# A selective-scan block with two layer norms and a linear attention: C's tails fetched a slot later, output offsets added two slots behind their products, a norm's third square kept out of two slots

## The chip, the cores and the metric

The kernel runs on one core of a Trainium2 chip. A core has a matrix engine (TensorE, PE in the profile; PEld is its loading of weights), a vector engine (DVE), an activation engine (ACT), a general engine (GpSimd, POOL) and a sync engine (SP), which here issues nearly all DMA transfers. Each engine works through its own instructions in order; semaphores order them against each other. The metric is device time in microseconds (us) of the whole kernel, median of several executions. Slot, step and group are the program's own words, explained below.

## The reference

The input x is 4 x 512 x 64 x 64. Two layers, each added to its input, each behind a group norm over 16 channels. The first is a Mamba block on four chunks of 128 channels; the second is a linear attention with 8 heads. Cut to what matters here:

```
def step(h, inp):                                   # 4096 positions, in order
    dt_t, B_t, C_t, x_t = inp
    dA = jnp.exp(dt_t[:, :, None] * A)
    h = dA * h + (dt_t * x_t)[:, :, None] * B_t[:, None, :]
    y = jnp.einsum('bds,bs->bd', h, C_t)            # 16 states, 256 channels
    return (h, y)
...
y = y * silu(z);  ym = out_proj(y) + skip * chunk
y = layer_norm(ym); x = x + y @ proj_w.T + proj_b
...
kq = einsum('bnhc,bnhd->bhcd', relu(k), relu(q))    # summed over all 4096 positions
out = (v @ kq / norm) @ w_out.T + b_out; x = x + out
```

## The kernel before

**Tiles and steps.** A tile is one batch element's 512 positions (32 tiles). A step is one chunk of 128 channels of a tile: 128 steps in order of batch, tile, chunk. A step has 256 inner channels (two halves `e`) of 16 states each; it is cut into 16 slots. Two slots, an even one (`jj` 0) and an odd one (`jj` 1), form a group: 4 states by 32 channels on the 128 partitions, four blocks of 32 channels next to each other in the free dimension, 512 positions each. There are 2,048 slots and 1,024 groups.

**A slot** (`slot`, from L835). POOL makes the drive `bx` = dt x times B for the slot after next (`drive`, L833). DVE runs two scans over time (L851); ACT makes the next decays `dA` (L825). In an even slot DVE multiplies the group before, its first 384 positions, by C out of PSUM (`product`, L871), and PE folds the states into `y` (`fold_states`). The last 128 positions, C's tail, are multiplied on POOL at the end of the odd slot (L863), behind the copy of the last state (L862), by `c_sb`, a broadcast of rows of C out of DRAM.

**Fetches.** `b_row` (even slots) issues four DMAs of 64 KB that broadcast the rows of B of the group three groups ahead; its tile has three buffers, so it waits until POOL's drives have read the old one. `c_tail` issues four DMAs of 16 KB for a tail; its tile `c_sb` has two buffers, so one may be filled while the other is read. Before the change it is called in the odd slot for the group that follows. Both issue through `for_states` (L800). SP also issues, from the `after` part of a slot, the spreads of dt and dt x (`spread`, two DMAs of 256 KB in each of slots 0 to 3 and 8 to 11, L752), the rows of dt (L739), of B and C (L771, L772), the 1 MB loads and stores of x tiles (L148, L542, L584) and the output's stores (L1144).

**After.** `after` is what a slot does besides: work with a fixed slot number, work put off by `later(n, ...)` until n slots on, and one piece each of three queues of generators: `ahead` (the norms before the scan), `late` (`leave`: the second layer norm and projection of a finished tile) and `rest` (the attention of a finished batch). A generator gives back a word at each `yield` that says when it may go on. `clear` holds a generator while the slot is one of `AWAY` (3 and 10, where ACT has the softplus and the silu with their table loads) or while more than one long ACT pass has been put into this slot. `room` holds it while PSUM work banks are taken: `held` counts them, and the limit is one in slots 1 to 5 and two elsewhere. The word "two ahead" is let through in slots 0, 1, 6 to 8 and 15.

**The norm behind the scan** (`layer_scale`). Four squares on ACT (L519), `part(0)` to `part(3)`, whose sums PE takes two by two. There is a `clear` before the first two and before the fourth; the third, `part(2)`, follows the sums of the first two at once.

**The attention's offset.** For batches 0 to 2, PE makes for each of four groups of output channels a product of 16 matmuls with one column (`pob`) in a work bank, and `offset` (L1102) adds it to the bias on DVE and frees the bank; it is put off by `later`. Behind all four come small additions on POOL (L1138), and then the attention's output (`pr`, stored through L1142). The last batch's attention runs behind the loop, in a branch of its own.

Of the kernel before, what the change touches and what calls it, by code (L numbers as in the profile page):

```python
# [24 lines left out]
def kernel(  # L25
# [53 lines left out]
    def work_bank(name, behind=1):  # L79
        held[0] += behind  # L80
        return ps_w.tile([P, T], F32, tag="w", name=name)

    def free(n=1):
        held[0] -= n

    def later(n, what):

        done = []

        def both():  # L90
            what()
            done.append(True)

        if now[0] is None:
            both()
        else:
            due.append((now[0] + n, both))
        return done
# [5 lines left out]
    def until(*done):  # L104
        while not all(done):
            yield "wait"

    def clear():

        while now[0] is not None and (now[0] % SLOTS in AWAY or passes[0] > 1):  # L110
            yield "wait" if now[0] % SLOTS in AWAY else "free"
# [4 lines left out]
    def room(when="wait"):  # L116

        while now[0] is not None and held[0] >= limit[0]:
            yield when
# [6 lines left out]
    def mm(out_, lhsT, rhs, abreast=1, **how):  # L126

        work["mm"] += (0.25 if rhs.dtype == BF16 else 1.0) * rhs.shape[-1] / T / abreast
        nc.tensor.matmul(out_, lhsT, rhs, **how)  # L129
# [276 lines left out]
    def bc(v, n):  # L406
        return v.unsqueeze(1).to_broadcast([P, n, v.shape[-1]])


    def sums_into(sums, parts, cs):  # L410
        for c in cs:
            mm(
                sums[c * LANE : (c + 1) * LANE, :], ones.to_broadcast([P, LANE]), parts[c],
                start=True, stop=True, abreast=len(cs),
            )

    def mean_of(sums, what, when, stop=True):

        got = wk.tile([P, T], F32, tag="sq", name=f"got_{what}", bufs=4)

        def take():
            nc.scalar.copy(got, sums)
            free()

        copied = later(1, take)
        yield
        yield from until(copied)
        yield when
        yield from room(when)
        bank = work_bank(what)  # L430
        mm(bank, mean.to_broadcast([P, P]), got, start=True, stop=stop)
        return bank
# [9 lines left out]
    def over_deviation(v, var, name):  # L442
        rs = wk.tile([P, T], F32, tag="sq", name=f"rs_{name}", bufs=4)

        def root():
            nc.scalar.activation(rs, var, AF.Ln, bias=eps)
            nc.scalar.activation(var, rs, AF.Exp, scale=-0.5)

        rooted = later(1, root)
        yield  # L450
        yield from until(rooted)
        yield "wide"
        over(v, var, ALU.mult)
        free()
        norming.clear()
        yield
# [38 lines left out]
    def layer_scale(v, name):  # L495


        while norming:
            yield "wait"
        norming.append(name)  # L500
        yield from room()
        sums = work_bank(f"mu_sums_{name}")
        sums_into(sums, [v[:, c, :] for c in range(NC)], range(NC))
        mu = yield from mean_of(sums, f"mu_{name}", None)
        mu2 = wk.tile([P, T], F32, tag="sq", name=f"mu2_{name}", bufs=4)

        def square():
            nc.scalar.activation(mu2, mu, AF.Square, bias=about)
            free()

        squared = later(1, square)
        yield
        yield from until(squared)
        sqs = [None] * NC

        def part(c):
            sqs[c] = wk.tile([P, T], F32, tag="sq", name=f"sq_{name}_{c}", bufs=4)
            passes[0] += 1
            nc.scalar.activation(sqs[c], v[:, c, :], AF.Square, bias=about)  # L519

        yield from clear()
        part(0)
        part(1)
        yield
        yield from room()
        sums = work_bank(f"var_sums_{name}")
        sums_into(sums, sqs, (0, 1))
        part(2)
        yield "free"
        yield from clear()  # L530
        part(3)
        yield "free"
        sums_into(sums, sqs, (2, 3))
        var = yield from mean_of(sums, f"var_{name}", "two ahead", False)
        mm(var, minus_first.to_broadcast([P, P]), mu2, start=False, stop=True)
        yield from over_deviation(v, var, name)
# [252 lines left out]
    def place(g):  # L789

        n, r = divmod(g, SLOTS)
        e, r = divmod(r, NQ * JJ)
        return n, e, *divmod(r, JJ)
# [3 lines left out]
    def for_states(dst, rows_, q):  # L797

        for k in range(KS):
            nc.sync.dma_start(  # L800
                dst[k * BLK : (k + 1) * BLK, :], rows_[q * KS + k, :].partition_broadcast(BLK)
            )

    def b_row(g):
        n, e, q, _ = place(g)
        b_all[g // JJ] = wk.tile([P, T], F32, tag="b_all", name=f"b_all_{g}", bufs=3)
        for_states(b_all[g // JJ], fs[n]["b_rows"], q)

    def c_tail(g):
        n, e, q, _ = place(g)  # L810
        c_sb[g // JJ] = wk.tile([P, T - CUT], F32, tag="c_sb", name=f"c_sb_{g}", bufs=2)
        for_states(c_sb[g // JJ], fs[n]["c_rows"], q)
# [7 lines left out]
    def decay(k):  # L820

        n, e, q, jj = place(k // 2)
        j = jj * 2 + k % 2
        dAs[k] = ps_d.tile([P, T], F32, tag="dA", name=f"dA_{k}")
        nc.scalar.activation(  # L825
            dAs[k], fs[n]["d_all", e][:, 0, j, :], AF.Exp, scale=a_t[:, e, j, q : q + 1]
        )

    def drive(g):

        n, e, q, jj = place(g)
        bxs[g] = wk.tile([P, 2, T], F32, tag="bx", name=f"bx_{g}", bufs=3)
        nc.gpsimd.tensor_tensor(  # L833
            bxs[g], fs[n]["d_all", e][:, 1, jj * 2 : jj * 2 + 2, :], bc(b_all[g // JJ], 2), ALU.mult
        )  # L835

    def slot(g, last, after):
        n, e, q, jj = place(g)
        b, t, c = steps[n]
        if g + 2 < last:  # L840
            drive(g + 2)
        if jj == 0:
            if g + 3 * JJ < last:
                b_row(g + 3 * JJ)
            hs[g // JJ] = wk.tile([P, NJ, T], F32, tag="h", name=f"h_{g}", bufs=2)
        elif g + 1 < last:
            c_tail(g + 1)
        h = hs[g // JJ]
        for i in range(2):
            j = jj * 2 + i  # L850
            nc.vector.tensor_tensor_scan(  # L851
                h[:, j, :], dAs.pop(2 * g + i), bxs[g][:, i, :],
                0.0 if t == 0 else st[:, c, e, q, j : j + 1], ALU.mult, ALU.add,
            )
            if 2 * g + i + LEAD < 2 * last:
                decay(2 * g + i + LEAD)
            if i == int(g % SLOTS == AWAY[1]) and jj == 0 and g:
                product(g - 1)
                fold_states(g - 1, last)
        del bxs[g]  # L860
        if jj == JJ - 1:
            nc.gpsimd.tensor_copy(st[:, c, e, q, :], h[:, :, T - 1])  # L862
            nc.gpsimd.tensor_tensor(  # L863
                h[:, :, CUT:], h[:, :, CUT:], bc(c_sb.pop(g // JJ), NJ), ALU.mult
            )
        after()

    def product(g):

        own = hs[g // JJ][:, :, :CUT]  # L870
        nc.vector.tensor_tensor(own, own, bc(c_all.pop(g // JJ), NJ), ALU.mult)  # L871
# [51 lines left out]
    def attention(b, x1s, stats):  # L923
# [5 lines left out]
        last = b == B - 1  # L929
# [123 lines left out]
        taken = []  # L1053
# [8 lines left out]
        for p in range(NC):  # L1062
            yield from room()
            pm = work_bank(f"pm2_{b}_{p}")
# [8 lines left out]
        taken = []  # L1073
# [10 lines left out]
        for m in range(NC):  # L1084
            yield from room()
            pm = work_bank(f"pm3_{b}_{m}")
# [12 lines left out]
        taken = []  # L1099

        def offset(o, pm):
            nc.vector.tensor_tensor(ob[:, o : o + 1], pm[:, 0:1], bo[:, o : o + 1], ALU.add)  # L1102
            free()
# [12 lines left out]
        for o in range(0 if last else NC):  # L1116
            yield from room()
            pm = work_bank(f"pob_{b}_{o}")
            for p in range(NC):
                mm(  # L1120
                    pm[:, 0:1], m2[:, p, o * P : (o + 1) * P], bv[:, p : p + 1],
                    start=(p == 0), stop=False,
                )
            for m in range(NC):
                mm(
                    pm[:, 0:1], m3[:, m, o * P : (o + 1) * P], ngm[:, m : m + 1],
                    start=False, stop=(m == NC - 1),
                )
            taken.append(later(1, lambda o=o, pm=pm: offset(o, pm)))
            yield  # L1130
        yield from until(*taken)
        free_x()
# [120 lines left out]
    wide, taken = 0, []  # L1253
# [208 lines left out]
```

## Time and profile before

| what | us |
|---|---|
| median of three runs | 7667.04 |
| the three runs | 7658.92 to 7670.27 |
| the profiled execution's own time | 7665.56 |
| its span, first to last instruction | 7663.9 |
| POOL: the drives, L833 | 4825.1 |
| POOL: the tails' product, L863 | 1301.2 |
| DVE: scans, L851 (both forms) | 4351.8 and 591.4 |
| DVE: product with C, L871 | 1771.0 |
| ACT: decays, L825 | 2752.5 |
| ACT: the squares of the norm behind the scan, L519 | 85.8 |

In a line for a group of instructions the columns are: source line, engine, operation, the tiles written and read, the shapes, the count, then busy time and the mean duration in ns of one, then the idle time of that engine just before such an instruction, and what ended most of it. In a line of the waits: who waited, for whom, the total in us, how many times, the longest. In the timeline: start, duration, engine, line, operation, tiles; in brackets the idle time before it and what ended it. A `q` after an engine's name means its sequencer, which issues transfers and waits.

### The profile page before, as it was taken

Reading aid. Unit: us, or ns where it says so; the run is one execution under the profiler, and the core shown is the slowest. Engines: PE = TensorE matmul, PEld = TensorE weight load, DVE = VectorE, ACT = ScalarE, POOL = GpSimd, SP = SyncE. Lnnn points to the kernel's source line nnn. Section 1 sums busy time; section 2 is a strip of 40 time slices with the busy share of each in tenths; the row PEclk is TensorE's granted clock in tenths of the full one; section 3 lists DMA queues with packets and bytes.
Section 4 is the critical chain, followed back from the end, with each engine's and each line's share of the span. In section 5 each row is a group of like instructions: output and inputs, shape, how many; then the busy total and the mean of one; then the engine's idle time right before and its main releaser. Section 6 shows DMA issues by size and latency. Waiting matters only on the chain.

```text
span 7663.9 us, 93895 instructions
## 1 busy us (share of the span) xinstructions
PE 6445.6 (84%) x25507; PEld 2129.9 (28%) x25528; DVE 6950.2 (91%) x5720; ACT 5455.4 (71%) x8384; POOL 6890.5 (90%) x4638
## 2 busy tenths in 40 slices
PE   5677777777798899998788889898789999899799
PEld 2122222121232233332222233332223333233244
DVE  6999999999999999899999999999999999999821
ACT  5677777777777777777777777777777777777521
POOL 5999999999999999999999999999999999999700
PEclk8787877787899999999799999999889999999899
DMA  6666666666666666676666666667676666677502
GB/s 173 170 172 165 160 152 162 161 162 167 178 168 167 168 172 167 170 195 181 172 178 171 177 168 170 162 177 209 164 169 166 163 160 162 172 189 192 146 34 93
DMA packets 829233, 1265.55 MB, mean 165 GB/s; under 512 B 184072, under 2 KB 317720, under 8 KB 816416
## 3 DMA queue, kind: packets, MB, share of 16 engines
q1 hardware_dynamic: 806352, 1225.99, 61.6%
q0 software_dynamic: 16368, 32.51, 2.5%
q8 instruction: 204, 3.34, 0.2%
q14 instruction: 325, 2.66, 0.1%
q10 hardware_dynamic: 5984, 1.06, 0.1%
HBM read 1052.25 MB, written 206.57 MB: 164 GB/s over the span
## 4 chain that ended last, share of the span: by engine, by line
PE 28%; DVE 23%; DMA 13%; ACT 12%; issue 9%; POOL 9%; SPq 5%; POOLq 0%; DVEq 0%; ACTq 0%
DVE h L851 14%; DVE h L871 7%; PE pc L129 7%; POOL bx L833 6%; ACT dA L825 5%; DMA d_all<-d_rows 5%; DMA c_sb<-c_rows 4%; PE pq L129 4%; PE y L129 4%; SPq L800 4%; PE pp L129 3%; PE pr L129 3%; PE po L129 2%; DMA b_all<-b_rows 2%; DVE xn L440 2%
## 5 line engine op out<-in xcount | busy, mean ns | idle before, releaser
L833 POOL TENSOR_TENSOR bx<-d_all,b_all 128x1024 f32<-128x1024 f32 x2048 | 4825.1, 2369 | 105.5 <-DVE h L851 85.9
L851 DVE TENSOR_TENSOR_SCAN h<-dA,st,bx 128x512 f32<-128x512 f32 x3584 | 4351.8, 1267 | 252.7 <-PE y L129 99.0
L825 ACT ACTIVATE dA<-d_all,a_t 128x512 f32<-128x512 f32 x4096 | 2752.5, 687 | 1274.0 <-DVE h L851 1194.4
L129 PE MATMUL y<-h,fold 128*32 128x512 f32 x8192 | 1267.8, 685 | 850.7 <-DVE h L871 472.0
L871 DVE TENSOR_TENSOR h<-h,c_all 128x1536 f32<-128x1536 f32 x1024 | 1771.0, 1730 | 0.1
L863 POOL TENSOR_TENSOR h<-h,c_sb 128x512 f32<-128x512 f32 x1024 | 1301.2, 1271 | 116.8 <-DMA c_sb<-c_rows 32.3
L129 PE MATMUL pc<-xn,w_cv 128*128 128x512 f32 x2048 | 1109.1, 673 | 151.6 <-DVE xn L440 100.8
L129 PE MATMUL pq<-w_qk,xa 128*128 128x512 f32 x2048 | 958.1, 602 | 4.4 <-ACT xa L398 2.5
L129 PEld LDWEIGHTS y<-h,fold 128*32 128x32 f32 x8192 | 186.2, 113 | 1702.2 <-POOL h L863 880.5
L851 DVE TENSOR_TENSOR_SCAN h<-dA,bx 128x512 f32<-128x512 f32 x512 | 591.4, 1206 | 36.1 <-POOL bx L833 20.6
L129 PEld LDWEIGHTS pc<-xn,w_cv 128*128 128x128 f32 x2048 | 412.5, 210 | 712.1 <-issue 430.7
L129 PEld LDWEIGHTS pq<-w_qk,xa 128*128 128x128 f32 x2048 | 391.5, 194 | 461.3 <-issue 438.6
L129 PE MATMUL pr<-xb,m 128*128 128x512 f32 x1024 | 479.4, 607 | 4.1 <-ACT res L1142 2.2
L129 PE MATMUL pp<-xn,w_pr 128*128 128x512 f32 x1024 | 477.4, 593 | 4.7 <-ACT xr L563 4.7
L129 PEld LDWEIGHTS <-sel 128*128 128x128 bf16 x1216 | 116.6, 97 | 1064.0 <-issue 1062.3
L129 PE MATMUL c_all<-parts,sel 128*128 128x384 bf16 x1024 | 374.4, 366 | 0.6 <-ACT parts L781 0.6
L129 PE MATMUL y<-xz,dg 32*32 32x512 f32 x2048 | 317.1, 691 | 32.5 <-ACT xz L891 32.0
L894 POOL TENSOR_TENSOR xz<-xz 128x512 f32<-128x512 f32 x256 | 326.6, 1276 | 4.6 <-ACT xz L891 4.6
L736 POOL TENSOR_TENSOR dt<-dt,xz 128x1024 f32<-128x1024 f32 x127 | 300.1, 2363 | 0.6 <-ACT dt L728 0.6
L129 PE MATMUL pd<-xz,w_xp 128*128 128x512 f32 x512 | 295.3, 708 | 0.0
L129 PE MATMUL pz<-xn,w_z 128*128 128x512 f32 x512 | 261.6, 598 | 7.4 <-ACT kq L965 2.4
L129 PEld LDWEIGHTS pr<-xb,m 128*128 128x128 f32 x1024 | 195.8, 195 | 251.4 <-issue 220.0
(226 smaller groups left out, 6044.3 us busy)
## 6 DMA issues: line engine op xcount, KB each, us to landing
d_all<-d_rows SPq DMA_DIRECT2D x2040, 256.0 KB, 4.4
b_all<-b_rows SPq DMA_DIRECT2D x4096, 64.0 KB, 2.5
d_rows<-dt SPq DMA_DIRECT2D x254, 512.0 KB, 3.0
c_sb<-c_rows SPq DMA_DIRECT2D x4096, 16.0 KB, 3.5
xn<-in_x_dram SPq DMA_DIRECT2D x32, 1024.0 KB, 8.5
x<-xr SPq DMA_DIRECT2D x32, 1024.0 KB, 4.8
xa<-x SPq DMA_DIRECT2D x32, 1024.0 KB, 5.3
xb<-x SPq DMA_DIRECT2D x32, 1024.0 KB, 5.3
```

Source lines behind the costliest of these rows:

```text
L129: nc.tensor.matmul(out_, lhsT, rhs, **how)
L440: nc.vector.tensor_tensor(v, v, bc(m, NC), op)
L736: nc.gpsimd.tensor_tensor(f["both"][:, 1], f["both"][:, 0], f["xz"][:, 0], ALU.mult)
L800: nc.sync.dma_start(dst[k * BLK : (k + 1) * BLK, :], rows_[q * KS + k, :].partition_broadcast(BLK))
L825: nc.scalar.activation(dAs[k], fs[n]["d_all", e][:, 0, j, :], AF.Exp, scale=a_t[:, e, j, q : q + 1])
L833: nc.gpsimd.tensor_tensor(bxs[g], fs[n]["d_all", e][:, 1, jj * 2 : jj * 2 + 2, :], bc(b_all[g // JJ], 2), ALU.mult)
L851: nc.vector.tensor_tensor_scan(h[:, j, :], dAs.pop(2 * g + i), bxs[g][:, i, :], 0.0 if t == 0 else st[:, c, e, q, j : j + 1], ALU.mult, AL ...
L863: nc.gpsimd.tensor_tensor(h[:, :, CUT:], h[:, :, CUT:], bc(c_sb.pop(g // JJ), NJ), ALU.mult)
L871: nc.vector.tensor_tensor(own, own, bc(c_all.pop(g // JJ), NJ), ALU.mult)
L894: nc.gpsimd.tensor_tensor(f["xz"][:, 1, e, :], f["xz"][:, 1, e, :], f["xz"][:, 0, e, :], ALU.mult)
```

## The change

The tail of a group is fetched in the even slot of the group itself, behind `b_row`, and no longer in the odd slot of the group before; the first group's is still fetched ahead of the loop. `offset` runs two slots behind its product, where it ran one behind. In `layer_scale` a `clear` stands before the third square, so that it is put into no slot of `AWAY` and into none that has two long passes already.

```diff
@@ layer_scale
         part(0)
         part(1)
         yield
+        yield from clear()
         yield from room()
         sums = work_bank(f"var_sums_{name}")
         sums_into(sums, sqs, (0, 1))
@@ slot
         if jj == 0:
             if g + 3 * JJ < last:
                 b_row(g + 3 * JJ)
+            if g:
+                c_tail(g)
             hs[g // JJ] = wk.tile([P, NJ, T], F32, tag="h", name=f"h_{g}", bufs=2)
-        elif g + 1 < last:
-            c_tail(g + 1)
         h = hs[g // JJ]
@@ attention
-            taken.append(later(1, lambda o=o, pm=pm: offset(o, pm)))
+            taken.append(later(2, lambda o=o, pm=pm: offset(o, pm)))
             yield
```

## The prediction

> **What bounds the kernel now.** First the page's shares and costliest groups, for which engines are full.
>
> ```profile
> PE 6445.6 (84%) x25507; PEld 2129.9 (28%) x25528; DVE 6950.2 (91%) x5720; ACT 5455.4 (71%) x8384; POOL 6890.5 (90%) x4638
> ...
> L833 POOL TENSOR_TENSOR bx<-d_all,b_all 128x1024 f32<-128x1024 f32 x2048 | 4825.1, 2369 | 105.5 <-DVE h L851 85.9
> L851 DVE TENSOR_TENSOR_SCAN h<-dA,st,bx 128x512 f32<-128x512 f32 x3584 | 4351.8, 1267 | 252.7 <-PE y L129 99.0
> ...
> L863 POOL TENSOR_TENSOR h<-h,c_sb 128x512 f32<-128x512 f32 x1024 | 1301.2, 1271 | 116.8 <-DMA c_sb<-c_rows 32.3
> ...
> c_sb<-c_rows SPq DMA_DIRECT2D x4096, 16.0 KB, 3.5
> xn<-in_x_dram SPq DMA_DIRECT2D x32, 1024.0 KB, 8.5
> ```
>
> DVE and POOL are both nearly full. The 91% mixes two stages, so next the sums by stretch: the slot loop (100 to 7240 us) and the attention of the last batch behind it.
>
> ```profile
> core 0: us, PE busy (x) PEld busy (x) DVE busy (x) ACT busy (x) POOL busy (x), PEclk, DMA share, GB/s
> 100.00:7240.00 7140.00, 5986.77 (x23964) 1922.92 (x23985) 6812.54 (x5414) 5340.49 (x8215) 6876.73 (x4618) 0.89 0.67 171
> ```
>
> In the loop POOL is busy 6876.7 of 7140 us and idle 263.3; DVE is idle 327.5. POOL sets the pace, DVE follows within 1%: whatever makes POOL wait has 263 us to hide in. All three edits act in the loop, so the tail (424 us) stays. Then the waits: POOL's idle time holds only 32.3 us (21 times) for `c_sb`, the tails that this change fetches later. Last, the waits of SP, which issues nearly every transfer, strictly in order:
>
> ```profile
> SPq L800 <- POOL st L862: 986.6, 629, 5.9
> SPq L800 <- DMA d_all<-d_rows: 293.1, 568, 2.8
> ...
> SPq L800 <- DMA xn<-in_x_dram: 114.9, 31, 5.5
> ...
> SPq L800 <- DMA xb<-x: 56.6, 22, 4.8
> ```
>
> The first row is `b_row` waiting until POOL has read the old buffer (the release is the end of a `bx`; the view names its neighbour `st`). The others look odd, since a fetch of B needs no x tile: SP's transfers take eight semaphores in turn, as their records show, so one waits until the eighth before it has landed. A 1 MB load thus stops SP for up to 5.5 us.
>
> **Edit 1, the tails.** Nothing is added or removed: 4,096 issues of 0.42 us on SP stay. A group's four move past the `after` part of the odd slot before (spreads, x loads, stores) and past the next `b_row`. Now they go out a full buffer ahead: from the first issue to the product at L863 the records give a median of 10.8 us. Afterwards they stand behind `b_row`, which waits for the `bx` of the slot before. One group, SP and POOL:
>
> ```profile
> 3015.02 1.69 SPq L800 DMA_DIRECT2D b_all<-b_rows  x4
> 3018.49 0.30 SPq L771 DMA_DIRECT2D b_rows<-dt  x1
> 3018.84 0.42 SPq L772 DMA_DIRECT2D c_rows<-dt  x1
> 3019.36 1.75 SPq L800 DMA_DIRECT2D c_sb<-c_rows  x4
> ```
>
> ```profile
> 3012.65 2.35 POOL L833 TENSOR_TENSOR bx<-d_all,b_all 128x1024 f32<-128x1024 f32 x1 [0.17 <-DVE h L851]
> ...
> 3016.48 2.37 POOL L833 TENSOR_TENSOR bx<-d_all,b_all 128x1024 f32<-128x1024 f32 x1
> 3019.01 2.36 POOL L833 TENSOR_TENSOR bx<-d_all,b_all 128x1024 f32<-128x1024 f32 x1 [0.17 <-DVE h L851]
> 3021.35 0.19 POOL L862 COPY st<-h 128x4 f32<-128x4 f32 x1
> 3021.62 1.27 POOL L863 TENSOR_TENSOR h<-h,c_sb 128x512 f32<-128x512 f32 x1
> ```
>
> The `bx` ends at 3015.00 and releases `b_row`; the next L863 starts 6.62 us later (of 1,000 such groups a third have 6.4 or less, least 6.32, median 6.95). In this time the new order needs `b_row` 1.8, the start of the fourth tail 1.4 later, and its landing: 1.8 to 2.0 us in slots without a spread, so 5.0 to 5.2. The spare time of a tight group falls to about 1.2 us. Where SP comes late by more, POOL waits.
>
> How often? For 1,000 groups I took from the records the end of the `b_row` that will stand before the tails, added the spacing that the four tail issues of that position show now (with their stalls) and a landing, compared it with the start of L863, and took out of a group's lag what the group before had already pushed POOL back. That gives 232 us of lateness for a landing of 1.5 us, 309 us in 202 groups for 2.0, 514 for 3.0, 719 for the page's median of 3.5 (which mixes in tails issued straight behind a spread; in the new order only B's rows are). It is bunched: 105 of the 309 us at slot 2, where SP waits for the xn load, 75 at slot 12, 53 at slot 6 behind the dt rows. I take 309, nearest to the slots without a spread, with 232 and 514 as ends. Check by the views: the five rows of 1 MB transfers (xn, xb, xs, xa, x) come to 280 us in 113 waits; less 1.2 us each that is 144, and the rest are groups where several lags add.
>
> The Trainium skill speaks against this edit: "DMA: Bandwidth & Descriptors", section "Rules for kernel authors", wants a DMA issued early and awaited late. Its section "Anatomy of one DMA" gives some 2.0 us fixed per DMA (for the other issuing path); with 16 KB that makes an estimate near my 2.0 and the same sum, where the row's 3.5 would make it 719.
>
> What a late L863 costs: queued behind it on POOL are the next `bx`, the gates and the dt product; PE, in order, waits at the fold of `y`; DVE's scans lie 1.3 to 4 us behind their `bx`, which absorbs a first shift, but POOL recovers only 2 us per step of 55.8. So count idle time. POOL now idles 263 us, 231 without the tails' 32. With 309 for the tails the idle time is at least 309 (all else vanishes: +46) and at most 309 + 231 (nothing vanishes: +277). The waits for DVE (85.9 at `bx`, 28.8 at `st`) are half of the 231 and go first when POOL is the late one, the others stay: 309 + 115 - 263 = **+161 us**.
>
> **Edit 2, the offsets.** Twelve small adds (L1102) of batches 0 to 2. In the loop DVE waits 21.8 us before six of them, since the products (16 matmuls, some 3.5 us at 0.22 each) are queued on PE behind others:
>
> ```profile
>   PE pob L129: 21.8, 6
> ...
> 3214.41 0.16 DVE L1102 TENSOR_TENSOR ob<-pob,bo 128x1 f32<-128x1 f32 x1 [6.46 <-PE pob L129]
> ```
>
> One slot more (about 3.5 us) ends the waits but for about 3 us in each of the two of 6.46: some 16 us. Against it a work bank is held a slot longer, so attention moves by a few slots three times; its last store in the loop, at 7167 us, leaves 73 us of cover. With the cover gone, a slot of 3.5 us each. POOL's 11.9 us before L1138 wait for the same products. Ends: +10 and -22; I take **-14**.
>
> **Edit 3, the square.** By counting the `dA` before each square of L519, 11 of 31 tiles have their third square in slot 10, beside the silu and its table loads; in no tile another pass stands before it in its slot, so only those 11 change. The square (0.72 us) and the fourth go into slot 11; the sums follow a slot later, which the wait for the window at slot 15 hides; without that cover the norm comes a step later. 11 x 0.72 = 8 us if all of it is exposed; +5 if slot 11 becomes the late one. I take **-4**.
>
> Sum: 161 - 14 - 4 = +143 on the profiled execution (span 7663.9, 1.7 us around it, 7665.56 in all, 1.5 below the median of three): 7665.6 + 143 = **7809 us**.
>
> **The rivals.**
> A, paid in full: tails land as slowly as behind a spread (lateness 514) and half the other idle time stays: 514 + 115 - 263 - 18 = +348, 8013 us. For it: PE already waits for L863 and would hand the delay to ACT's copies. Against: the spreads move behind the tails.
> B, hidden: DVE and PE set the pace and POOL's waits only replace its waits for DVE; +46 - 18, and less where longer periods give SP its spare time back: 7665 to 7680 us, within 0.2% at its middle. Against: 115 us of such waits cannot hold 309.
> C, faster: the tails are in time because, moved ahead of the spreads and loads of their slot, they no longer stand behind them in the queue, and what is left is the offsets' 21.8 us on DVE in the first slots of three steps and the 8 us of squares: about -25, 7641 us. It decides if lateness stays below some 30 us, as much as now. For it: 800 of 1,000 groups have spare time. Against: the xn load stops the same semaphores whatever the order.
> D, the squares' edit moves nothing: it costs 4 us of the sum.
>
> **How the numbers follow.** No change means within 0.2% (15 us), about what a measurement can tell. Forecast 0.58 (own range 7710 to 7890); A 0.14; B 0.11; C 0.17, with D inside all. So slower 0.72, same 0.11, faster 0.17. The range takes in C's middle and the forecast, and leaves most of A out: 7636 to 7940.
>
> **What would show it.** L863's idle time on `c_sb` up from 32 to 250 to 350 us, most at slots 3, 7 and 13; POOL's wait for DVE halved; the wait on `pob` below 10 us. If the `c_sb` wait stays under 60 us, the lateness count is wrong and C holds; if it is there and the span does not grow, the hiding (B) was misjudged.

## The result, and the profile after

The changed kernel takes 8064.2 us (median of five runs, 8055.7 to 8070.47) against 7667.04 us. The ratio is 1.0522, 95% interval 1.0511 to 1.0534: some 400 us slower. The forecast had the direction and the place, but put the loss at 143 us, and its range ended at 7940.

In the profile after, line numbers below the added `clear` are one higher: the tails' product is L864, the drive L834. First the page, costliest groups and transfers:

```profile
PE 6512.8 (81%) x25507; PEld 2137.1 (27%) x25528; DVE 6972.4 (86%) x5720; ACT 5464.1 (68%) x8384; POOL 6869.0 (85%) x4638
...
L834 POOL TENSOR_TENSOR bx<-d_all,b_all 128x1024 f32<-128x1024 f32 x2048 | 4813.6, 2367 | 33.1 <-DVE h L852 20.5
...
L864 POOL TENSOR_TENSOR h<-h,c_sb 128x512 f32<-128x512 f32 x1024 | 1298.2, 1268 | 642.3 <-DMA c_sb<-c_rows 569.5
...
d_all<-d_rows SPq DMA_DIRECT2D x2040, 256.0 KB, 4.9
b_all<-b_rows SPq DMA_DIRECT2D x4096, 64.0 KB, 4.4
...
c_sb<-c_rows SPq DMA_DIRECT2D x4096, 16.0 KB, 2.0
```

No engine has more work to do. L864 costs what L863 did, but POOL now stands idle 569.5 us in front of it for `c_sb`, where it stood 32.3. The landing of a tail became shorter, as forecast (2.0 us in place of 3.5), but that of B's rows longer (4.4 in place of 2.5): a first hint that something changed on SP's queue that the forecast did not have. The row of B before:

```profile
b_all<-b_rows SPq DMA_DIRECT2D x4096, 64.0 KB, 2.5
```

The loop, now 400 us longer (100 to 7640 us):

```profile
core 0: us, PE busy (x) PEld busy (x) DVE busy (x) ACT busy (x) POOL busy (x), PEclk, DMA share, GB/s
100.00:7640.00 7540.00, 6056.85 (x23964) 1931.19 (x23988) 6833.44 (x5413) 5348.57 (x8214) 6854.05 (x4618) 0.88 0.64 162
```

POOL is idle 7540 - 6854.05 = 686 us, of which 569.5 are the tails and 116.5 all else. Before it was 263.3, of which 32.3 and 231. The waits of the changed kernel, in the loop's engines and then on SP:

```profile
POOL h L864 <- DMA c_sb<-c_rows: 569.5, 282, 10.2
DVE h L852 <- POOL bx L834: 467.9, 338, 8.9
PE y L129 <- POOL h L864: 883.8, 397, 8.5
```

```profile
SPq L801 <- DMA d_all<-d_rows: 1158.3, 1403, 3.4
SPq L801 <- POOL st L863: 923.1, 610, 4.5
...
SPq L801 <- DMA xn<-in_x_dram: 109.6, 31, 5.7
```

DVE's wait for `bx` went from 71.7 (in the loop) to 467.9 us: it now follows at a distance. On SP the row of the xn loads is as before (114.9), but that of the spreads grew from 293.1 us in 568 waits to 1158.3 in 1403. Of these, 1150 us in 1384 waits stand in front of tail issues (90 us in 191 waits before; the expectation of `tails_ahead` below has 1177 and 80). SP's timeline shows what happens, first in the kernel before, then in the changed one:

```profile
3001.06 1.76 SPq L800 DMA_DIRECT2D b_all<-b_rows  x4
3002.86 0.90 SPq L752 DMA_DIRECT2D d_all<-d_rows  x2
3003.86 1.81 SPq L800 DMA_DIRECT2D c_sb<-c_rows  x4
3005.71 0.90 SPq L752 DMA_DIRECT2D d_all<-d_rows  x2
3008.42 2.00 SPq L800 DMA_DIRECT2D b_all<-b_rows  x4
```

```profile
3177.05 1.79 SPq L753 DMA_DIRECT2D d_all<-d_rows  x4
3179.56 1.70 SPq L801 DMA_DIRECT2D b_all<-b_rows  x4
3181.31 3.44 SPq L801 DMA_DIRECT2D c_sb<-c_rows  x4
3184.80 1.85 SPq L753 DMA_DIRECT2D d_all<-d_rows  x4
3186.96 1.70 SPq L801 DMA_DIRECT2D b_all<-b_rows  x4
3188.70 3.70 SPq L801 DMA_DIRECT2D c_sb<-c_rows  x4
```

Before, a group's tails went out between the spread of the even slot and that of the odd slot (two transfers each). With the tails moved up, the two spreads stand side by side, four transfers of 256 KB, and behind them come B's four rows and the four tails. SP's transfers use eight semaphores in turn, so each tail waits until the spread eight places ahead of it has landed: the issue of the four tails takes 3.4 to 3.7 us and not 1.8. From the end of the `bx` that releases `b_row` to the issue of the fourth tail the records give 3.2 us (median) at slot 0, but 6.1, 6.6, 5.2 and 6.1 at slots 2, 4, 10 and 12, which follow a spread.

### The profile page after: what moved, and what is told of

Same layout as the page of the kernel before. It is cut to its first block, busy times and chain, and to the rows that moved or that the text cites. A ratio compares the mean times of both kernels' runs of the same rounds, so it can differ in the third digit from the quotient of the medians.

```text
span 8062.5 us, 92137 instructions
## 1 busy us (share of the span) xinstructions
PE 6512.8 (81%) x25507; PEld 2137.1 (27%) x25528; DVE 6972.4 (86%) x5720; ACT 5464.1 (68%) x8384; POOL 6869.0 (85%) x4638
## 4 chain that ended last, share of the span: by engine, by line
DMA 33%; PE 17%; DVE 13%; POOL 11%; SPq 11%; issue 8%; ACT 8%; POOLq 0%; DVEq 0%; ACTq 0%
DMA d_all<-d_rows 20%; DVE h L852 8%; POOL bx L834 6%; SPq L801 6%; DMA c_sb<-c_rows 5%; SPq L753 4%; DVE h L872 4%; PE pc L129 4%; PE pq L129 4%; ACT dA L826 3%; POOL h L864 3%; PE y L129 3%; DMA b_all<-b_rows 3%; PE pr L129 2%; PE po L129 1%
## 5 line engine op out<-in xcount | busy, mean ns | idle before, releaser
L834 POOL TENSOR_TENSOR bx<-d_all,b_all 128x1024 f32<-128x1024 f32 x2048 | 4813.6, 2367 | 33.1 <-DVE h L852 20.5
L129 PE MATMUL y<-h,fold 128*32 128x512 f32 x8192 | 1289.4, 701 | 1216.3 <-POOL h L864 883.8
L864 POOL TENSOR_TENSOR h<-h,c_sb 128x512 f32<-128x512 f32 x1024 | 1298.2, 1268 | 642.3 <-DMA c_sb<-c_rows 569.5
L129 PE MATMUL pq<-w_qk,xa 128*128 128x512 f32 x2048 | 976.8, 612 | 5.4 <-ACT xa L398 2.5
```

Source lines behind the costliest of these rows:

```text
L834: nc.gpsimd.tensor_tensor(bxs[g], fs[n]["d_all", e][:, 1, jj * 2 : jj * 2 + 2, :], bc(b_all[g // JJ], 2), ALU.mult)
L864: nc.gpsimd.tensor_tensor(h[:, :, CUT:], h[:, :, CUT:], bc(c_sb.pop(g // JJ), NJ), ALU.mult)
```

## The experiments

**Which edit.** `tails_only` is the kernel before with edit 1; `rest_only` has edits 2 and 3 and not edit 1; `offset_only` and `clear_only` have one of these each.

> Edit 1 alone, on the kernel before. If the whole loss is the tails' (the trace after shows POOL idle 569.5 us for c_sb before L864, against 32.3), this kernel is as slow as the changed one or, without the other two edits' small gain, a little slower: 8065 to 8095 us, with the wait for c_sb at 540 to 600 us. If the other edits cost something, it is faster than the changed kernel: below 8040.

Measured: 8061.27 us, 1.051 (1.0494 to 1.0526).

```profile
POOL h L863 <- DMA c_sb<-c_rows: 571.9, 274, 8.6
```

That is POOL's wait in `tails_only`, as in the changed kernel (569.5). The whole loss is edit 1's.

> Edits 2 and 3 without edit 1: the tails are fetched as before. By the prediction's own terms (-14 and -4 us) 7649 us, ratio 0.9977. If the longer hold of the work banks or the later sums cost, 7675 or more. DVE's wait for pob in the loop should fall from 21.8 us to under 6.

Measured: 7658.48 us, 0.9992 (0.9982 to 1.0001): 6 us, where 18 were forecast, and not clear of no change.

> Edit 2 alone on the kernel before. By the prediction -14 us (7652 us); since rest_only showed both small edits together at 0.9992, I now expect -3 us, from 0.9980 to 1.0010, with DVE's wait for pob in the loop at 1 to 6 us in place of 21.8.

Measured: 7667.13 us, 1.0006 (0.9997 to 1.0015): edit 2 gains nothing, though its wait is gone. DVE's waits in the loop, without edit 2 and then in `offset_only`:

```profile
DVE h L851 <- PE y L129: 109.0, 104, 3.1
DVE h L851 <- ACT dA L825: 82.8, 131, 3.1
DVE h L851 <- POOL bx L833: 71.7, 83, 4.2
DVE ob L1102 <- PE pob L129: 21.8, 6, 6.5
```

```profile
DVE h L851 <- PE y L129: 100.4, 102, 3.1
DVE h L851 <- POOL bx L833: 93.9, 88, 6.3
DVE h L851 <- ACT dA L825: 90.7, 136, 2.2
```

Of the 21.8 us for `pob` 1.4 are left, and the wait for POOL's `bx` has grown by 22.2. This fits a wait that was handed on, DVE getting there sooner and finding POOL not ready, but the one row doesn't show it: POOL's own wait for the tails also grew in this run, from 32.3 to 44.2 us, and it differs as much between other kernels that fetch their tails alike (48.0 in `clear_only`). Shown is that 20 us less of DVE's waits left the time where it was.

> Edit 3 alone on the kernel before. By the prediction -4 us; from 0.9985 to 1.0010, within what can be told from no change. The eleven squares in slot 10 should stand in slot 11.

Measured: 7650.94 us, 0.9981 (0.9972 to 0.999): some 16 us faster, more than the 4 us of the forecast. In the kernels that have edit 2 as well such a gain doesn't show: `rest_only` above gains 6 us, and `rest_c_one` below is 1 us faster than `c_one_only`. By the count of decays before each square, no square stands in slot 10; of the 11 tiles nine now have the third and fourth in slot 11, and two have them in slots 13 and 14.

**Distance or order.** Edit 1 does two things: it shortens the distance from a tail's issue to its use (from the issue of the fourth tail to its product, median of the records: 9.2 us before, 2.9 after), and it changes the order on SP's queue. Three kernels, all with edits 2 and 3, take these apart.

`tails_ahead`, the changed order with about the old distance (8.2 us):

```diff
             if g + 3 * JJ < last:
                 b_row(g + 3 * JJ)
-            if g:
-                c_tail(g)
+            if g + JJ < last:
+                c_tail(g + JJ)
```

> All three edits, with the changed kernel's place and order on SP's queue (behind b_row in the even slot), but the tails of the next group, not of this one, so that they have a group more to land. SP should still be stopped by the spreads' landing, as in the changed kernel (its trace: 1177 us before tail issues, against 80 before): if these stops cost only because the tails are late, the time is 7640 to 7700 us and POOL's wait for c_sb under 60. If the stops of SP cost by themselves (b_all and d_all late too), the time stays 100 us or more above the kernel before.

Measured: 7749.41 us, 1.0109 (1.0095 to 1.0122). The stops of SP are as long as in the changed kernel, POOL's wait for the tails is back to its size before, and another has come. SP's row, and then POOL's:

```profile
SPq L801 <- DMA d_all<-d_rows: 1146.7, 1418, 2.7
```

```profile
POOL bx L834 <- DMA d_all<-d_rows: 100.7, 54, 5.2
...
POOL h L864 <- DMA c_sb<-c_rows: 29.4, 16, 7.9
```

So both expectations were half right: most of the loss needs the short distance, and the order alone costs 1.1% over the kernel before, for SP now issues the spreads too late for `bx` (why, `ahead_one` below asks).

`tails_between`, a short distance (4.0 us) with the old order, the call moved behind the slot's own work:

```diff
-            if g:
-                c_tail(g)
...
         after()
+        if jj == 0 and g:
+            c_tail(g)
```

> All three edits, the tails fetched for their own group in the even slot, but behind that slot's spread and not ahead of it: the short distance of the changed kernel with the order on SP's queue of the kernel before (B, spread, tails, spread). It takes the order's part away and leaves the distance. SP's stops before tails and B on spreads should fall from 1158 to 200 to 350 us. By the records of the kernel before (end of the tails' issue, landing of 3.9 to 4.3 us behind a spread), the distance alone makes 1180 us of lateness in 629 of 999 groups, so the time should be 8250 to 8750 us. If the order made the changed kernel's loss, this one is faster than it: below 8000.

Measured: 8298.83 us, 1.0824 (1.0809 to 1.0838), inside the expected span. SP, then POOL:

```profile
SPq L801 <- DMA d_all<-d_rows: 215.0, 442, 2.9
```

```profile
POOL h L862 <- DMA c_sb<-c_rows: 824.2, 350, 10.8
```

The stops fall to 215 us, and POOL waits more than ever, since the tails go out behind the slot's own work and, in a slot with a spread, land behind it: the fourth in 3.6 to 4.0 us (medians), elsewhere in 1.8. The distance is the main cost in either order. The count from the records (1180 us) was too high here.

`tails_first`, the tails ahead of `b_row` in the same slot:

```diff
         if jj == 0:
+            if g:
+                c_tail(g)
             if g + 3 * JJ < last:
                 b_row(g + 3 * JJ)
-            if g:
-                c_tail(g)
```

> All three edits, but in the even slot the tails of the group are issued ahead of b_row, so that they need not wait for POOL's bx (their own buffer was read two groups ago) and go out as soon as SP is through with the slot before. If the loss comes from standing behind b_row's wait and behind the spreads that take the same semaphores (eight in turn: the tails' eighth predecessors are then B's rows, long landed), POOL's wait for c_sb falls to 30 to 80 us and the time to 7640 to 7690 us. If fetching in the group's own slot is too late as such, it stays above 7850.

Measured: 7779.05 us, 1.0146 (1.0132 to 1.0159), some 90 us above the span that I expected. POOL's waits:

```profile
POOL h L864 <- DMA c_sb<-c_rows: 136.3, 68, 9.2
POOL h L864 <- DMA b_all<-b_rows: 75.9, 41, 7.3
```

Freed from `b_row`'s wait, the fourth tail goes out on average 0.45 us after the end of the `bx` (5.26 in the changed kernel), which wins back nearly three quarters of the loss. But it stands behind four spreads in a row and lands after 4.9 to 5.3 us (medians) at the slots that follow one (1.8 elsewhere). SP's stops on the spreads are still there (1104.2 us), now in front of `b_row`. L864 reads no B; why the view names B's rows for 75.9 us stays open.

**The stops on the semaphores.** If SP's stops made the wait larger than counted, fewer transfers between tail and spread should bring it back. `tails_one_dma` is the changed kernel with four rows in one DMA:

```diff
-        for_states(c_sb[g // JJ], fs[n]["c_rows"], q)
+        rows_ = fs[n]["c_rows"][q * KS : (q + 1) * KS, :]
+        nc.sync.dma_start(
+            c_sb[g // JJ], rows_.unsqueeze(1).to_broadcast([KS, BLK, T - CUT])
+        )
```

> The changed kernel, with a group's four tails in one DMA of 64 KB and not in four of 16 KB: three issues of 0.42 us and three turns of the semaphores fewer per group; the tail's eighth predecessor is then the first spread of the even slot, the earliest of the four to land. If SP's stops on the spreads' semaphores made the wait 569 us and not the 309 us that I counted without them, it falls to 100 to 309 us and the time to 7700 to 7810 us. If it is the landing beside the spreads (3.0 to 3.7 us and not 1.8 to 2.0) that made it, the wait stays above 400 us and the time above 7900. A slow landing of a DMA with a broadcast in it would spoil the reading; its landing time will show that.

Measured: 7840.21 us, 1.0227 (1.0213 to 1.0241). POOL, and then SP (L814 is the tails' issue):

```profile
POOL h L867 <- DMA c_sb<-c_rows: 281.3, 142, 7.3
```

```profile
SPq L814 <- DMA d_all<-d_rows: 60.3, 88, 1.7
```

The stops on spreads are down to 60.3 us at the tails; 203.5 now stand at the spreads' own issue (L753). The wait is 281.3 us and the time 173 us above the kernel before. The forecast had 309 us and +143 for a kernel without stops. The time is 30 us over what I expected; other waits of POOL stayed larger (454 us idle in its loop of 100 to 7420 us, so 173 beside the tails'). The one DMA also saves three issues of 0.42 us, which this run doesn't separate from the stops. By the updates of its semaphore it lands 3.2 us after its issue (median), about as late as four undisturbed tails do, counted from the first issue (1.35 + 1.8).

`ahead_one` makes the same edit to `tails_ahead`:

> As tails_ahead (all three edits, the next group's tails behind b_row in the even slot; 7749 us, POOL waiting 94 us for d_all), but a group's four tails in one DMA. If the 85 us that tails_ahead costs come from SP's stops on the spreads' semaphores, which make the next spreads late, they go with the stops: 7635 to 7675 us and POOL's wait for d_all under 20 us. If they come from the four spreads standing side by side in the transfer queues, the time stays above 7720.

Measured: 7622.98 us, 0.9943 (0.9928 to 0.9959). POOL's waits:

```profile
POOL bx L837 <- DVE h L855: 83.6, 196, 2.4
...
POOL bx L837 <- DMA d_all<-d_rows: 3.9, 3, 2.9
POOL h L867 <- DMA c_sb<-c_rows: 3.4, 2, 1.9
```

Four spreads still stand side by side, and the wait for `d_all` is gone. So it came from SP being late: from its stops (on spreads 208.9 us at L753 and 105.1 at L740, where `tails_ahead` had 1146.7) or from the three issues per group that are saved here too; this run doesn't separate the two. This is the fastest kernel of the study. Against `rest_c_one` below, which has the tails where they were before, POOL waits 3.4 us for them and not 27.1, and the time is 19 us less.

The same edit with the tails where they were before, without and with edits 2 and 3:

> The kernel before with nothing changed but a group's four tails in one DMA. rest_c_one (this with edits 2 and 3) was 0.9968 of the kernel before, rest_only (edits 2 and 3) 0.9992. If the one DMA makes the gain, 7640 to 7652 us here, ratio 0.997 to 0.998. If edits 2 and 3 are needed for it, within 0.1% of the kernel before.

Measured: 7642.88 us, 0.9973 (0.9964 to 0.9981).

> Edits 2 and 3, tails fetched as before, but a group's four tails in one DMA of 64 KB. If the stops of SP on semaphores cost something in the kernel before as well (its trace: some 290 us on spreads and 280 us on 1 MB transfers), they become rarer with 9 in place of 12 DMAs per group in the slots with spreads: POOL's wait for c_sb below 25 us and the time 7630 to 7655. If they lie in cover, 7650 to 7670. A slow landing of the one DMA shows as a longer wait for c_sb and a time above 7700.

Measured: 7641.81 us, 0.9968 (0.9955 to 0.998). The one DMA makes the gain; edits 2 and 3 add nothing that these intervals show.

`rest_both_one` makes one DMA of B's four rows as well:

> As the last, with B's four rows in one DMA of 256 KB too: 6 DMAs per group. SP's stops on spreads and on 1 MB transfers should all but go (eight DMAs are more than a group), so 7620 to 7650 us if they cost, 7650 to 7670 if not. A slow landing of the large one would show in POOL's wait for b_all.

Measured: 8398.49 us, 1.0959 (1.0939 to 1.0978), a clear miss. POOL, and three of SP's rows:

```profile
POOL h L870 <- DMA c_sb<-c_rows: 766.5, 377, 8.1
```

```profile
SPq L753 <- DMA b_all<-b_rows: 536.4, 240, 4.6
SPq L817 <- DMA b_all<-b_rows: 268.1, 88, 5.3
SPq L809 <- DMA b_all<-b_rows: 245.6, 163, 3.9
```

SP, hardly ever held by B's rows before, now stops more than 1000 us for the large DMA's landing, and the tails and spreads behind it are late. The records of the semaphores say more. A DMA of one row updates its semaphore 16 times as it lands. A DMA of four rows gives five updates: one about 1 us after its issue, four with its data. For B's these four come 9.4 to 11.7 us after the issue (medians; a row of B landed in 2.5 before). Size alone isn't it: a spread before, 256 KB too and with 16 updates, landed in 4.4. In this run a spread has twelve of its updates within 4.4 us, but the last four only after 9.2 to 11.4. Both fit a DMA of four rows that runs through 4 of 16 engines and holds up what queues behind it there. The Trainium skill has such a rule ("DMA: Bandwidth & Descriptors", section "Rules for kernel authors": an outermost dimension of fewer than 16 confines a DMA to at most so many engines), and these counts agree with it; no run here has B's four rows in one DMA of another shape.

## Why the prediction was wrong

- **What bounds the kernel.** Right. POOL sets the pace, and its idle time made the loss.
- **The form of the sum.** Right. I wrote the tails' wait, plus half of the other 231 us of idle time, less 263. The other idle time came out at 116.5 us (115 forecast), though in part by luck: the waits for DVE did not vanish but fell from 114.7 to 36.7 us, and the rest, which was to stay, fell from 116.3 to 79.8. With the measured wait: 569.5 + 116.5 - 263.3 = +422.7, less 22.7 us of POOL's busy time, is the 400 us by which the loop grew.
- **The lateness count: the step that failed.** The term that was wrong is the issue of the four tails. I gave them "the spacing that the four tail issues of that position show now", which belonged to the old order. The move also took the tails out from between the spreads. At slots 2, 4, 10 and 12 four spreads in a row now stand ahead of `b_row`, the tails take their semaphores, and the four issues spread over 3.3 to 4.3 us (means) in place of 1.35 (median before). The other term, a landing of 2.0 us, held: the fourth tail, which lands last, takes 1.7 us at these slots (medians) and 2.0 on average in the groups where POOL waits. The first tail takes 4.4 to 5.0 us there, but nothing waits for it alone. Done again on the records of the kernel before, with a landing of 2.0 us, such a count gives some 300 us with the old spacing, and some 580 when the spacing of the changed kernel is put in and nothing else is changed. Measured were 569.5. Without most of the stops (`tails_one_dma`) it was 281.
- **"The spreads move behind the tails"**, my argument against rival A, was true inside a group and false for the next. I had read the rule of the eight semaphores from the trace and applied it to the xn loads alone.
- **Rival A** came nearest (8013 us), but by luck: it had the tails land later, and the tail that counts landed as forecast. The excess was late issue.
- **Rival B, hidden, and C, faster,** are out: 569.5 us of waits don't fit into POOL's idle time. C's thought that tails ahead of the spreads no longer stand behind them missed the same point.
- **Edit 2** was forecast at -14 us and shows no gain (1.0006). I had given POOL the pace and yet counted an idle time of DVE as a gain; which wait took its place is not shown.
- **Edit 3** was forecast at -4 us and measures about -16 alone (-8 to -21 by its interval), but nothing that the intervals show beside edit 2. The most that I had allowed it was 8 us; what a square in slot 10 holds up was not traced.
- **Where it shows.** By L864's idle time on `c_sb`, slots 3 (219 us) and 13 (240) lead, as said; slot 7, also named, has 27 us, with no spread ahead of it.
- The rule of the Trainium skill that spoke against the edit ("DMA: Bandwidth & Descriptors", section "Rules for kernel authors": issue early, wait late) held: the same order with a group more of distance (`tails_ahead`) gives back 315 of the 400 us. The fixed cost of some 2.0 us that its section "Anatomy of one DMA" gives, for the other issuing path, is near what undisturbed tails take here (1.8 us).

## What to carry to other kernels

When a transfer is moved on an in-order queue, write out the new order for two periods and count semaphore turns in it: what was between two large transfers and leaves brings them together, and whatever comes eight places behind them stops. A wait of the engine that follows need not be a gain when removed (1.0006 here for edit 2); count the idle time of the engine that sets the pace. Fewer and larger transfers on such a queue can pay without touching any engine's work (0.9973 here for one edit), but not where the large one lands late (1.0959).

## What the runs showed of the hardware that was not expected

- SP's transfers share eight semaphores in turn, and with spreads of 256 KB ahead this held SP for some 1150 us of an 8060 us kernel, although the transfer engines were busy only 64% of the loop.
- A 16 KB broadcast landed in 1.8 us undisturbed and, as the fourth tail directly behind four spreads of 256 KB, in 4.9 to 5.3 us (`tails_first`). With B's four rows between them, the four tails of the changed kernel landed in 4.4 to 5.0, 3.8 to 3.9, 2.7 to 2.8 and 1.7 us: each had been held by SP until one more spread was in.
- A DMA of four rows gave 5 updates of its semaphore, a spread 16; with 256 KB in each such DMA, the last four of a spread's 16 updates came 9.2 to 11.4 us after its issue, the first twelve within 4.4.
